# A three-layer interaction network in float32: the order of the first loads, and how the last eight samples are pooled

## The chip, the cores and the metric

The kernel runs on one core of one Trainium2 chip. The metric is the device time of one execution in microseconds (us); the time before is the median of three runs.

## The reference

The input `x` holds 1024 samples of 64 features by 16 embedding elements (`e`). Each of three layers multiplies every feature of `x` with every channel of the hidden state, element by element of `e`, and contracts all products with a weight matrix. Half of the outputs of layers 0 and 1 goes on as the hidden state, the other half to the end; there everything is added up over `e` and weighted with one vector into one number for each sample.

```python
x0 = h = x                                   # [1024, 64, 16]
for i in range(3):
    z = einsum('bfe,bge->bfge', x0, h).reshape(B, f0 * fh, 16)
    y = einsum('oc,bce->boe', W[i], z) + b[i][None, :, None]   # 128 outputs
    x_i, h = (y[:, :64], y[:, 64:]) if i < 2 else (y, y)
    xs.append(x_i)
pooled = sum(concatenate(xs, axis=1), axis=2)                  # [1024, 256]
return pooled @ fc_w.T + fc_b                                  # [1024, 1]
```

Since the end is linear, the kernel folds `fc_w` into the weights: `V2` (from `W2` and its part of `fc_w`), then `V1` and `V0`, and a constant. Each sample's result is a sum over 64 rows and 16 elements of products `uu`, plus the constant.

## The kernel before

**Tiling.** The samples are cut into 32 chunks of `CB = 32`; a chunk is `N = 512` columns, sample by sample with 16 elements each. Two chunks, an even and an odd one, share a pair `k`: the even one has rows 0 to 63, the odd one rows 64 to 127. For a chunk, `product` makes four tiles `z` (index `j`, [128, 4, 512]) by multiplying `xa` (x's rows, four shifts of them, 1 MB) with a column block of `x`, on VectorE (DVE), now and then on GpSimd (POOL). `contract` then runs 16 matmuls of [128 x 128] weights `w_all` with 512 columns into a PSUM accumulator, each of them two passes in float32. `factors` copies one half of the accumulator with ScalarE (ACT, L332) and multiplies it with the other half on DVE (L338) into `uu[:, 0]`; V0's part of the pair is `uu[:, 1]`, made earlier by `x_v0x`. `sums` (L347) adds `uu` over `e` into `acc` [128, 2, 16, 32], and `pool` adds `acc` over rows with a matmul whose stationary operand `ones` [128, 2] has one column for each half of the rows (L612).

**Order.** The order of each engine's instructions is the order of the program text; nothing is scheduled by a planner. Each engine works its list in that order, and so do the DMA queues of SP (SyncE) and ACT. Consecutive DMAs, of both queues, take eight completion semaphores in turn, so a DMA can only be issued when the one eight before it has landed.

**The head.** The weights of the third layer need layer 1's output of four chunks first (`HEAD = [2, 3, 0, 1]`, here `c0` to `c3`), and meanwhile the folded matrix is made from `W2` and `W1`. TensorE (PE) starts with matmuls on zeros (L106). All loads of the head are issued by SP: `xa` of c0 in a first quarter (two halves of 64 rows), a second quarter and the rest; `wh`, block 0 of W0 (`w0t[:, 0]`, 256 KB); the first quarter of c1; the other three blocks of W0 (`w0r`, L182, one block and then two); the vectors `vs` (L183, 100 KB); the rest of c1; then W2 in two halves of 1 MB (L188), W1 (L189) and c2.

- For c0 and c1 the second factor is not loaded but shifted out of `xa`'s first quarter by PE (`shift_pair`, L205). The pair (0, 1) reads the upper 64 rows for j = 0 and the lower 64 for j = 1.
- `h1_weights(j)` (L355) makes block j of `w_all` on DVE: it adds two halves of W0's block j, one of which ACT has copied to PSUM (L365 for block 0, L374 for block 1, L379 for blocks 2 and 3).
- c0's z of j = 1 is made by POOL in pieces, the others by DVE. DVE's order is: block 0 of the weights, z of j = 0 in pieces (i = 0, i = 1, i = 2 and 3), half of z of j = 2, block 1 of the weights, the rest of j = 2, blocks 2 and 3, z of j = 3.
- PE's order (`half_contract`, L298): tiles i = 0 and 1 of j = 0, c1's shifts (0, 3), tiles 2 and 3, j = 1, c1's shifts (1, 2), j = 2 and 3; then `pv` (L413), a product of W2 with `fv2` (32 copies of one column of `vs`, copied by ACT at L398), for each half of W2; then c1's contraction, of which the folded matrix `pm` (L437) is a neighbour.

**The tail.** The last chunk, 31, has its accumulator in two pieces: `CUT = 24` samples (384 columns) and 8 samples (128 columns). After the first piece its factors and sums run while PE contracts the second. After the second piece one chain of small steps follows: ACT's copy (L332), DVE's multiplication (L338), DVE's sum over e (L347), PE's pool (L612), DVE's addition of the constant `cst` (L623), and a DMA of the pair's 64 results by SP (L624).

Of the kernel before, what the change touches and what calls it, by code (L numbers as in the profile page):

```python
# [49 lines left out]
NCH = B // CB  # L50
NI = 4
NJ = 4
NT = NI * NJ
XR = 128 + NI
# [10 lines left out]
def cin_kernel(ctx, tc, xra, xrb, wh, w0r, w1h, w2t, wx1, wx0, vec, out):  # L65
    nc = tc.nc
# [22 lines left out]


    vs = const_tile("vs", [128, NV])
    fc2, bh1, bh2 = vs[:, 0:1], vs[:, 1:2], vs[0:64, 2:3]
    bcol, fcol, fcb = vs[:, 3:5], vs[:, 5:7], vs[:, 7:8]
    w0ds, fcr = vs[:, 8:72], vs[:, 72:200]

    fv2 = const_tile("fv2", [128, 32])

    v0w = const_tile("v0w", [128, 2, F])
    v1w = const_tile("v1w", [128, 2, F])
# [2 lines left out]


    zeros = nc.const_aps.tensor(0.0, [128, 128])
    for n in (128,) * 5 + (64,):
        nc.tensor.matmul(misc[:, 0:n], zeros, zeros[:, 0:n], start=True, stop=True)  # L106

    shift = const_tile("shift", [128, 96])
# [7 lines left out]
    ones = const_tile("ones", [128, 2])  # L116
# [9 lines left out]
    res = const_tile("res", [128, 128])  # L126


    xas, xbs, xxs, xrs, sqs = {}, {}, {}, {}, {}

    def load_xa(c, at=slice(0, NI), rows=slice(0, 128)):
        if at.start == rows.start == 0:
            xas[c] = xp.tile([128, NI, N], F32, tag="xa", name=f"xa_{c}")
        nc.sync.dma_start(  # L134
            out=xas[c][rows, at, :],
            in_=bass.AP(
                tensor=xra.tensor, offset=(c * XR + rows.start + at.start) * N,
                ap=[[N, rows.stop - rows.start], [1, (at.stop - at.start) * N]],
            ),
        )  # L140

# [29 lines left out]
    c0, c1, c2, c3 = HEAD  # L171
    w0t = z_tile("w0t")
    w2s = [flat_tile(f"w2_{k}") for k in range(2)]
    w1s = set_tile("w1s")
    for rows in halves:
        load_xa(c0, slice(0, 1), rows)
    nc.sync.dma_start(out=w0t[:, 0, :], in_=wh)  # L177
    load_xa(c0, slice(1, 2))
    load_xa(c0, slice(2, 4))
    load_xa(c1, slice(0, 1))  # L180
    for at in (slice(0, 1), slice(1, NJ - 1)):
        nc.sync.dma_start(out=w0t[:, at.start + 1 : at.stop + 1, :], in_=w0r[:, at])  # L182
    nc.sync.dma_start(out=vs, in_=vec)  # L183
    load_xa(c1, slice(1, 4))
    w0s = [w0t[:, j, :].rearrange("p (i v g) -> p i v g", v=2, g=F) for j in range(NJ)]
    xb_gps = xp.tile([128, NJ, N], F32, tag="xb", name="xb_gps")
# [20 lines left out]
                    xas[c][halves[r], 0, :], start=True, stop=True,  # L207
                )

    for j, tag in ((1, "y"), (0, "y"), (2, "set"), (3, "acc")):  # L210
        shifted(c0, j, tag)
    shift_pair(c0, (0, 1))
    shift_pair(c0, (2, 3))
# [31 lines left out]
    def tiles(j):  # L245

        return (1, 2, 3, 0) if j == NJ - 1 else range(NI)
# [42 lines left out]
                    )  # L290


    def half_contract(c, *js, last=None, at=None):
        for j in js:
            for i in at or tiles(j):
                t = j * NI + i
                for n in range(2):
                    nc.tensor.matmul(  # L298
                        accs[c][halves[n]], w_all[:, t, 0:64],
                        zs[c, j][:, i, n * H2 : (n + 1) * H2],  # L300
                        start=(t == 0), stop=(j == last and i == tiles(j)[-1]),
                    )
# [42 lines left out]
    def sums(k, rows=slice(0, 128), of=slice(0, 2), half=slice(0, CB)):  # L345

        nc.vector.tensor_reduce(  # L347
            acc[rows, of, k, half],
            uus[k][rows, of, E * half.start : E * half.stop].rearrange("p k (b e) -> p k b e", e=E),
            AX.X,  # L350
            ALU.add,
        )
# [27 lines left out]
    nc.vector.memset(w0o[3][SQ, 0, :], 0.0)  # L380
    for j in (2, 3):
        h1_weights(j, w0o[j])
    half_contract(c0, 0, at=(0, 1))


    for j, tag in ((0, "y"), (3, "acc"), (1, "y"), (2, "set")):
        shifted(c1, j, tag)
    shift_pair(c1, (0, 3))
    half_contract(c0, 0, at=(2, 3))
    half_contract(c0, 1)  # L390
    shift_pair(c1, (1, 2))
    new_acc(c1, H2)
# [2 lines left out]

    product(c0, 3)
    load_chunk(c3)
    nc.scalar.copy(fv2, fc2.to_broadcast([128, 32]))  # L398
    half_contract(c0, 2, 3, last=3)
    keep_h1(c0)  # L400

# [8 lines left out]
    for n in range(2):  # L410
        pv = ps.tile([128, 512], F32, tag=("set", "y")[n], name=f"pv2_{n}")
        for k in range(4):
            nc.tensor.matmul(  # L413
                pv[32 * k : 32 * k + 32], fv2, w2s[n][:, k * 512 : (k + 1) * 512],
                start=True, stop=True,
# [6 lines left out]
    for h in range(2):  # L422
        at = slice(32 * h, 32 * h + 32)
# [40 lines left out]
    for half, queue in enumerate((nc.sync, nc.scalar)):  # L464
        queue.dma_start(
            out=m_ap(0, 32 * half, [[row, F], [1, 32 * F]]), in_=m_rows[halves[half]]
# [5 lines left out]
        out=m_ap(64, 68, [[row, 4], [4 * F, 7], [1, 4 * F]]),  # L472
        in_=m_rows[0:4, 4 * F :].rearrange("p (k c) -> p k c", c=4 * F),
# [79 lines left out]
        head_q(0, j)  # L553

    cst = const_tile("cst", [128, 1])
    made = set()

    def load_products(c, other=None):
# [46 lines left out]
    NP = NCH // 2  # L605
    QP = NP // 4
# [7 lines left out]
            tile_position=(0, 32 * g), skip_group_check=True, **flags,  # L614
        )

    def finish(k0, k1, queue, engine=nc.scalar):
        g, at = k0 // QP, slice(k0 % QP, (k1 - 1) % QP + 1)
        rows = slice(32 * g, 32 * g + 2)
        if engine is nc.scalar:  # L620
            engine.activation(res[rows, at, :], po[rows, at, :], AF.Identity, bias=cst[rows])
        else:
            engine.tensor_scalar(res[rows, at, :], po[rows, at, :], cst[rows], None, ALU.add)  # L623
        queue.dma_start(out=outs[:, k0:k1, :], in_=res[rows, at, :])  # L624


# [1 line left out]
    for s, c in enumerate(order):  # L628
        k, head = c // 2, c in HEAD
        if order[s - 1] in HEAD and not head:  # L630
            for n in range(NF // 2):
                x_v0x(n)
            for n in HEAD:
                factors(n)
                if n % 2:
                    sums(n // 2)
        if 0 < s < len(order) - 2 and s not in (2, 3):
            load_products(*order[s + 2 : s + (4 if s == 6 else 3)])
        if s in (2, 3):

            if s == 2:
                for n in order[4:6]:
                    load_chunk(n)
                load_shared(0)
            for j in (0, 1) if s == 2 else (2, 3):
                for n in order[4:6]:
                    product(n, j)
        if s == len(HEAD) + 5:

            pc = ps.tile([128, 1], F32, tag="set", name="pc")  # L650
            for j in range(2):
                nc.tensor.matmul(
                    pc, fcol[:, j : j + 1].to_broadcast([128, 128]), bcol[:, j : j + 1],
                    start=(j == 0), stop=(j == 1),
                )
            nc.scalar.activation(cst, pc, AF.Identity, bias=fcb, scale=float(E))
        if not head:
            if c % 4 < 2:
                new_acc(c)
            if c == NCH - 1:  # L660
                factors(c - 1)
                sums(k, of=slice(1, 2))
                sums(k, slice(0, 64), slice(0, 1))
# [12 lines left out]
        elif c % 2:  # L676
            for n in (c - 1, c):
                new_acc(n)
            for j in range(NJ):
                head_q(k, j)  # L680
            contract_shared(0)
        if c % 4 == 1 and not head:
            for n in (1, 2):
                new_acc(c + n)
            contract_shared(c - 1)
        if s == 0:
            v0_weights()
            load_products(order[2], order[3])

        if c == HEAD[0] or c % 4 in (0, 3) and s and order[s - 1] not in HEAD and c < NCH - 1:  # L690
            factors(order[s - 1])
            if order[s - 1] % 2:
                sums(order[s - 1] // 2)
        elif c % 4 == 2 and not head:
            factors(c - 2)
            factors(c - 1)
            x_v0x(k - 1)
            x_v0x(k)
            sums(k - 1)


    first, last = slice(0, CUT), slice(CUT, CB)
    factors(NCH - 1)
    sums(NP - 1, slice(64, 128), slice(0, 1), first)
    for j in range(NJ):
        contract(NCH - 1, j, 1)
    factors(NCH - 1, slice(1, 2))
    sums(NP - 1, slice(64, 128), slice(0, 1), last)
    pool(NP - 1, NP, start=False, stop=True)
    finish(NP - 1, NP, nc.sync, nc.vector)  # L710


# [69 lines left out]
```

## Time and profile before

| what | value |
|---|---|
| time, median of 3 runs | 485.92 us (485.56 to 486.34) |
| time of the profiled execution | 485.56 us |
| span in its profile | 483.8 us |
| PE busy | 478.6 us, 99% of the span |
| DVE, ACT, POOL busy | 369.0, 67.0, 15.4 us |
| granted TensorE clock of the core, mean | 1.00 |
| data moved | 87.01 MB, 180 GB/s on average |

The profile shows one execution. Its span begins and ends with the program's instructions on the core; the rest of the execution's time, 485.56 - 483.8 = 1.8 us, lies around it. Times in the views count from the start of the span. A group "x8" of the timeline is eight instructions merged; "[0.60 <-DMA xa<-in_xra]" after one says that its engine was idle for 0.60 us before it and what ended that. A float32 matmul is recorded as two.

### The profile page before, as it was taken

The numbers are of one execution on the slowest core, as the hardware profiler recorded it, in microseconds if no ns is written. First come the engines' busy times: TensorE is split into PE (matmuls) and PEld (weight loads), VectorE is DVE, ScalarE is ACT, GpSimd is POOL, SyncE is SP. The second block draws the span as 40 slices with busy tenths as digits, with TensorE's granted clock in tenths as the row PEclk, the third lists the DMA queues.
The fourth block names the chain that finished last, engine by engine and source line by source line (L and its number), as shares of the span: only waits on it lengthen the run. The fifth ranks groups of instructions, "written<-read, shape, count | busy, mean of one in ns | idle before, by whom it ended". The sixth has DMA issues, their size and how long they took to land.

```text
span 483.8 us, 4411 instructions
## 1 busy us (share of the span) xinstructions
PE 478.6 (99%) x1800; PEld 215.4 (45%) x1800; DVE 369.0 (76%) x228; ACT 67.0 (14%) x141; POOL 15.4 (3%) x16
## 2 busy tenths in 40 slices
PE   8999999999999999999999999999999999999997
PEld 4465344443344444444444444444444444444555
DVE  4994799998899988898877686767878677771321
ACT  3242033111120111001000010001000010000001
POOL 5330000000000000000000000000000000000000
PEclk9999999999999999999999999999999999999999
DMA  7996996653951782587237344463346631000000
GB/s 279 415 310 196 389 384 261 229 205 120 354 234 75 239 293 108 198 268 280 110 128 215 159 173 173 152 211 110 136 173 208 225 127 49 0 1 0 0 1 1
DMA packets 19818, 87.01 MB, mean 180 GB/s; under 512 B 4850, under 2 KB 5522, under 8 KB 10902
## 3 DMA queue, kind: packets, MB, share of 16 engines
q1 hardware_dynamic: 18886, 85.81, 49.3%
q10 hardware_dynamic: 912, 0.92, 0.7%
q8 instruction: 14, 0.23, 0.2%
q14 instruction: 6, 0.05, 0.0%
HBM read 85.08 MB, written 1.64 MB: 179 GB/s over the span
## 4 chain that ended last, share of the span: by engine, by line
PE 95%; DMA 2%; SPq 1%; issue 0%; DVE 0%; ACT 0%
PE acc L257 80%; PE acc L316 6%; PE acc L298 4%; PE acc L273 3%; DMA w<-in_w2t 2%; PE acc L286 1%; SPq L134 1%; PE pm L437 0%; PE y L278 0%; PE pv L413 0%; SPq L182 0%; SPq L177 0%; PE po L612 0%; SPq L188 0%; SPq L183 0%
## 5 line engine op out<-in xcount | busy, mean ns | idle before, releaser
L257 PE MATMUL acc<-z,w_all 128*128 128x512 f32 (+2 forms) x928 | 387.6, 579 | 0.0
L235 DVE TENSOR_TENSOR z<-xa,xb 128x2048 f32<-128x2048 f32 x124 | 278.4, 2286 | 42.6 <-PE acc L257 36.3
L257 PEld LDWEIGHTS acc<-z,w_all 128*128 128x128 f32 x928 | 173.1, 190 | 213.0 <-issue 206.7
L240 ACT ACTIVATE z<-xa 32x512 f32<-32x512 f32 x34 | 21.3, 625 | 337.2 <-DVE z L235 335.2
L338 DVE SCALAR_TENSOR_TENSOR uu<-acc,vs,q 64x512 f32<-64x512 f32 (+2 forms) x29 | 21.2, 731 | 57.8 <-ACT q L332 57.6
L298 PE MATMUL acc<-z,w_all 128*64 128x256 f32 x256 | 28.8, 381 | 0.0
L316 PE MATMUL acc<-z,w_all 128*64 128x512 f32 x128 | 27.9, 593 | 0.0
L332 ACT COPY q<-acc 64x512 f32<-64x512 f32 (+2 forms) x33 | 18.7, 566 | 35.9 <-PE acc L257 19.8
L298 PEld LDWEIGHTS acc<-z,w_all 128*64 128x64 f32 x256 | 18.0, 137 | 11.8 <-issue 1.6
L235 DVE TENSOR_TENSOR z<-xa,xp 128x2048 f32<-128x2048 f32 (+2 forms) x12 | 20.4, 1749 | 0.6 <-DMA xa<-in_xra 0.6
L347 DVE TENSOR_REDUCE acc<-uu 128x64 f32<-128x1024 f32 (+4 forms) x19 | 20.3, 1073 | 0.3
L316 PEld LDWEIGHTS acc<-z,w_all 128*64 128x64 f32 x128 | 9.1, 137 | 18.0 <-issue 17.9
L278 PE MATMUL y<-xr,v0w 32*64 32x512 f32 x128 | 15.9, 600 | 0.0
L273 PE MATMUL acc<-xr,v1w 32*64 32x512 f32 (+2 forms) x132 | 15.7, 587 | 0.0
L343 DVE SCALAR_TENSOR_TENSOR uu<-y,cx,xx 128x512 f32<-128x512 f32 x16 | 11.3, 747 | 0.2
L235 POOL TENSOR_TENSOR z<-xa,xb_gps 128x512 f32<-128x512 f32 (+2 forms) x4 | 9.4, 2379 | 5.8 <-ACT xb_gps L367 4.9
L273 PEld LDWEIGHTS acc<-xr,v1w 32*64 32x64 f32 x132 | 5.1, 131 | 10.0 <-issue 9.8
L286 PE MATMUL acc<-sq,w_sq 32*64 32x512 f32 (+2 forms) x132 | 8.7, 574 | 0.0
L205 PE MATMUL xp<-xa,shift 64*64 64x512 f32 x32 | 5.8, 762 | 0.7 <-DMA xa<-in_xra 0.6
L165 ACT ACTIVATE sq<-xr 128x512 f32<-128x512 f32 x8 | 5.0, 630 | 3.0 <-DMA xr<-in_xra 2.8
L286 PEld LDWEIGHTS acc<-sq,w_sq 32*64 32x64 f32 x132 | 3.7, 132 | 3.7 <-issue 3.5
L355 DVE TENSOR_TENSOR w_all<-w0t,w0p 128x256 f32<-128x256 f32 x2 | 0.8, 419 | 5.8 <-ACT w0p L365 5.8
(57 smaller groups left out, 67.9 us busy)
## 6 DMA issues: line engine op xcount, KB each, us to landing
xa<-in_xra SPq DMA_DIRECT2D x32, 1024.0 KB, 5.0
xb<-in_xrb SPq DMA_DIRECT2D x31, 1024.0 KB, 7.3
xr<-in_xra SPq DMA_DIRECT2D x32, 128.0 KB, 7.7
xx<-in_xra SPq DMA_DIRECT2D x32, 128.0 KB, 7.7
w<-in_w2t SPq DMA_DIRECT2D x2, 1024.0 KB, 10.5
w1s<-in_w1h SPq DMA_DIRECT2D x1, 1024.0 KB
w1x<-in_wx SPq DMA_DIRECT2D x1, 1024.0 KB
w0x<-in_wx SPq DMA_DIRECT2D x1, 1024.0 KB, 5.5
```

The lines of the kernel that those rows point to most:

```text
L235: engine.tensor_tensor(zs[c, j][:, at, :], xas[c][:, at, :], xbs[c][j].unsqueeze(1).to_broadcast([128, last - first, N]), ALU.mult,)
L240: nc.scalar.activation(zs[c, j][SQ, 0, :], xas[c][SQ, 0, :], AF.Square)
L257: nc.tensor.matmul(acc_c, w_all[:, t, w_cols(c)], zs[c, j][:, i, cols], start=(t == 0 and c % 4 < 2), stop=(t == NT - NI and c % 4 >= 2),)
L273: nc.tensor.matmul(acc_c[halves[1 - n]], v1w[at, m], xr[:, cols], start=(m == 0 and c not in ends), stop=False, tile_position=(at.start, 6 ...
L278: nc.tensor.matmul(ys[c // 2][halves[n]], v0w[at, m], xr, start=(m == 0), stop=(m == 1), tile_position=(at.start, 64 * n),)
L286: nc.tensor.matmul(acc_c[halves[n]], w_sq[at, w_cols(c)][:, 64 * n : 64 * n + 64], sqs[first][at, cols], start=h and (first == 0 or c not ...
L298: nc.tensor.matmul(accs[c][halves[n]], w_all[:, t, 0:64], zs[c, j][:, i, n * H2 : (n + 1) * H2], start=(t == 0), stop=(j == last and i == ...
L316: nc.tensor.matmul(accs[c][halves[1 - c % 2]], w_all[:, t, 64:128], zs[c, j][:, i, :], start=(t == 0), stop=False,)
L332: nc.scalar.copy(q[h, cols], acc_c[64 - h.start : 128 - h.start])
L338: nc.vector.scalar_tensor_tensor(uu[:, cols], acc_c[h], bh1[h], q[h, cols], ALU.add, ALU.mult)
L343: nc.vector.scalar_tensor_tensor(uu_tile(k)[:, 1, :], ys[k], cx, xxs[k], ALU.add, ALU.mult)
L347: nc.vector.tensor_reduce(acc[rows, of, k, half], uus[k][rows, of, E * half.start : E * half.stop].rearrange("p k (b e) -> p k b e", e=E), ...
```

## The change

In the head:

- the vectors are loaded by ACT's DMA queue as the program's first DMA, and ACT's copy of `fv2`, which waits for them, becomes ACT's first copy (before: vectors on SP's queue behind W0, the copy behind c0's z);
- x's first quarter is loaded by one DMA in place of two, and W0's blocks 1 to 3 by one in place of two;
- one more matmul on zeros of 128 columns;
- PE contracts all four tiles of c0's j = 0 ahead of c1's shifts (0, 3), in place of two before them and two behind.

In the tail:

- rows 64 to 127 of `acc` for the last 8 samples are set to zero by POOL, so that the last `pool` holds only 24 samples of chunk 31. It no longer waits for the second piece. ACT adds the constant, and the pair's results go out in two DMAs: the even chunk's 32, and the odd chunk's first 24;
- the last 8 samples go another way: three matmuls with one stationary column add `uu[:, 1]` (V0's part), the constant (`csl`, the constant divided by 128 * 16, made once by ACT) and last `uu[:, 0]` over the rows, for 128 columns, into a [1, 128] accumulator `pl`; DVE then adds `pl` over e into 8 results, and a third DMA writes them.

```diff
     vs = const_tile("vs", [128, NV])
+    nc.scalar.dma_start(out=vs, in_=vec)
...
     fv2 = const_tile("fv2", [128, 32])
+    nc.scalar.copy(fv2, fc2.to_broadcast([128, 32]))
...
-    for n in (128,) * 5 + (64,):
+    for n in (128,) * 6 + (64,):
         nc.tensor.matmul(misc[:, 0:n], zeros, zeros[:, 0:n], start=True, stop=True)
...
-    for rows in halves:
-        load_xa(c0, slice(0, 1), rows)
+    load_xa(c0, slice(0, 1))
     nc.sync.dma_start(out=w0t[:, 0, :], in_=wh)
     load_xa(c0, slice(1, 2))
     load_xa(c0, slice(2, 4))
     load_xa(c1, slice(0, 1))
-    for at in (slice(0, 1), slice(1, NJ - 1)):
-        nc.sync.dma_start(out=w0t[:, at.start + 1 : at.stop + 1, :], in_=w0r[:, at])
-    nc.sync.dma_start(out=vs, in_=vec)
+    nc.sync.dma_start(out=w0t[:, 1:NJ, :], in_=w0r)
     load_xa(c1, slice(1, 4))
...
-    half_contract(c0, 0, at=(0, 1))
+    half_contract(c0, 0)
...
     shift_pair(c1, (0, 3))
-    half_contract(c0, 0, at=(2, 3))
     half_contract(c0, 1)
     shift_pair(c1, (1, 2))
...
     load_chunk(c3)
-    nc.scalar.copy(fv2, fc2.to_broadcast([128, 32]))
...
+    csl = const_tile("csl", [128, 1])
+    nc.gpsimd.memset(acc[64:128, 0, NCH // 2 - 1, CUT:], 0.0)
...
             nc.scalar.activation(cst, pc, AF.Identity, bias=fcb, scale=float(E))
+            nc.scalar.activation(csl, cst, AF.Identity, scale=1.0 / (128 * E))
...
-    first, last = slice(0, CUT), slice(CUT, CB)
+    first, last = slice(0, CUT), slice(E * CUT, N)
     factors(NCH - 1)
     sums(NP - 1, slice(64, 128), slice(0, 1), first)
     for j in range(NJ):
         contract(NCH - 1, j, 1)
     factors(NCH - 1, slice(1, 2))
-    sums(NP - 1, slice(64, 128), slice(0, 1), last)
     pool(NP - 1, NP, start=False, stop=True)
-    finish(NP - 1, NP, nc.sync, nc.vector)
+    pl = ps.tile([1, N - E * CUT], F32, tag="acc", name="pl", bufs=4)
+    uu = uus[NP - 1]
+    nc.tensor.matmul(pl, ones[:, 1:2], uu[:, 1, last], start=True, stop=False)
+    nc.tensor.matmul(
+        pl, csl, nc.const_aps.tensor(1.0, [128, N - E * CUT]), start=False, stop=False
+    )
+    nc.tensor.matmul(pl, ones[:, 1:2], uu[:, 0, last], start=False, stop=True)
+    rows, (even, odd) = slice(96, 98), (outs[0:1, NP - 1], outs[1:2, NP - 1])
+    nc.scalar.activation(
+        res[rows, QP - 1], po[rows, QP - 1], AF.Identity, bias=cst[rows]
+    )
+    nc.sync.dma_start(out=even, in_=res[96:97, QP - 1])
+    nc.sync.dma_start(out=odd[:, first], in_=res[97:98, QP - 1, first])
+    rl = hb[0:1, 0, 0 : CB - CUT]
+    nc.vector.tensor_reduce(rl, pl.rearrange("p (b e) -> p b e", e=E), AX.X, ALU.add)
+    nc.sync.dma_start(out=odd[:, CUT:], in_=rl)
```

More of the change, by code (lines that the diff above doesn't have):

```diff
@@ L129, in cin_kernel, with load_xa @@
     xas, xbs, xxs, xrs, sqs = {}, {}, {}, {}, {}
-    def load_xa(c, at=slice(0, NI), rows=slice(0, 128)):
-        if at.start == rows.start == 0:
+    def load_xa(c, at=slice(0, NI)):
+        if c not in xas or at.start == 0:
             xas[c] = xp.tile([128, NI, N], F32, tag="xa", name=f"xa_{c}")
         nc.sync.dma_start(
-            out=xas[c][rows, at, :],
+            out=xas[c][:, at, :],
             in_=bass.AP(
-                tensor=xra.tensor, offset=(c * XR + rows.start + at.start) * N,
-                ap=[[N, rows.stop - rows.start], [1, (at.stop - at.start) * N]],
+                tensor=xra.tensor, offset=c * XR * N + at.start * N,
+                ap=[[N, 128], [1, (at.stop - at.start) * N]],
             ),
@@ L208, in shift_pair @@
                 )
-    for j, tag in ((1, "y"), (0, "y"), (2, "set"), (3, "acc")):
+    for j, tag in enumerate(("y", "y", "set", "acc")):
         shifted(c0, j, tag)
@@ L290, in contract_shared, with half_contract @@
                     )
-    def half_contract(c, *js, last=None, at=None):
+    def half_contract(c, *js, last=None):
         for j in js:
-            for i in at or tiles(j):
+            for i in tiles(j):
                 t = j * NI + i
@@ L615, in pool, with finish @@
         )
-    def finish(k0, k1, queue, engine=nc.scalar):
+    def finish(k0, k1, queue):
         g, at = k0 // QP, slice(k0 % QP, (k1 - 1) % QP + 1)
         rows = slice(32 * g, 32 * g + 2)
[L620 to L623, printed above, removed]
+        nc.scalar.activation(
+            res[rows, at, :], po[rows, at, :], AF.Identity, bias=cst[rows]
+        )
         queue.dma_start(out=outs[:, k0:k1, :], in_=res[rows, at, :])
@@ L707, in cin_kernel @@
     factors(NCH - 1, slice(1, 2))
-    sums(NP - 1, slice(64, 128), slice(0, 1), last)
     pool(NP - 1, NP, start=False, stop=True)
-    finish(NP - 1, NP, nc.sync, nc.vector)
+    pl = ps.tile([1, N - E * CUT], F32, tag="acc", name="pl", bufs=4)
[6 more added lines that the diff above has]
+    rows, (even, odd) = slice(96, 98), (outs[0:1, NP - 1], outs[1:2, NP - 1])
+    nc.scalar.activation(
+        res[rows, QP - 1], po[rows, QP - 1], AF.Identity, bias=cst[rows]
+    )
+    nc.sync.dma_start(out=even, in_=res[96:97, QP - 1])
[3 more added lines that the diff above has]
+    nc.sync.dma_start(out=odd[:, CUT:], in_=rl)
 def kernel(r_x, L0_rec_W0, L0_rec_b0, L0_rec_W1, L0_rec_b1, L0_rec_W2, L0_rec_b2, L0_rec_fc_w, L0_rec_fc_b):
```

## The prediction

> **What bounds the kernel.** The page says at once what counts: PE is busy all through.
>
> ```profile
> PE 478.6 (99%) x1800; PEld 215.4 (45%) x1800; DVE 369.0 (76%) x228; ACT 67.0 (14%) x141; POOL 15.4 (3%) x16
> ```
>
> So I asked where PE still waits. The list of PE's waits between 19.5 and 480 us is empty, and the starts of its matmuls show no hole there. A gain or loss of the change must therefore lie before 19.7 us or after 480.1 us, and whatever PE gains by 19.7 us comes through whole. In the timeline of PE I read the head:
>
> ```profile
> 7.21 1.08 PE L298 MATMUL acc<-z,w_all 128*64 128x256 f32 x8
> 8.90 1.09 PE L205 MATMUL xp<-xa,shift 64*64 64x512 f32 x8 [0.60 <-DMA xa<-in_xra]
> 9.91 2.88 PE L298 MATMUL acc<-z,w_all 128*64 128x256 f32 x24
> 12.73 1.09 PE L205 MATMUL xp<-xa,shift 64*64 64x512 f32 x8
> ...
> 17.35 1.07 PE L413 MATMUL pv<-w,fv 128*32 128x512 f32 x8
> 18.72 1.07 PE L413 MATMUL pv<-w,fv 128*32 128x512 f32 x8 [0.30 <-DMA w<-in_w2t]
> ```
>
> PE has little to do until 9.9 us and is full from there, but for W2's second half, which lands at 18.6. A half of `pv` takes 0.91 us (its eight passes begin every 0.43 to 0.45 us in fours), so PE would have been ready at 17.35 + 0.91 = 18.26 and lost 18.72 - 18.26 = 0.46 us. Behind 9.91 the eight instructions of tiles 2 and 3 end at 10.6; j = 1 begins at 10.85, when block 1 of the weights is there. Its chain is in ACT's and DVE's timelines:
>
> ```profile
> 9.49 0.38 ACT L374 COPY w0p<-w0t 128x256 f32<-128x256 f32 x1 [2.48 <-DMA w0t<-in_w0r]
> 10.72 0.79 ACT L379 COPY misc<-w0t 128x256 f32<-128x256 f32 x2 [0.85 <-DMA w0t<-in_w0r]
> ```
> ```profile
> 10.29 0.42 DVE L355 TENSOR_TENSOR w_all<-w0t,w0p 128x256 f32<-128x256 f32 x1
> ```
>
> Block 1 lands at 9.43, blocks 2 and 3 at 10.71. What the DMAs do meanwhile is in the DMA view of the first 40 us (1 us a column):
>
> ```profile
> DMA  0057999999999999999999999999987979974037
> GB/s 0 0 154 217 377 342 350 229 401 419 415 444 408 459 418 418 426 434 410 426 418 383 338 438 426 438 434 410 442 246 164 246 238 279 205 229 162 14 64 179
> ```
>
> From 4 us to 28 us they are full: landings go by bytes, not by issue times. Between 2.2 us (first packet) and 4.5 us they are not: by half microseconds the packets fill 0.14 of 0.28, then 0.37, 0.35, 0.38 and 0.44 of 0.50 us, so 0.6 us of transfer time is unused, because SP issues one DMA per 0.62 us there. Last, the tail, in the chain of waits:
>
> ```profile
> 480.42 0.37 DVE uu L338
> 480.79 0.02 issue
> 480.81 0.29 DVE acc L347
> 481.11 0.14 issue
> 481.24 0.23 PE po L612 x2
> 481.47 0.03 issue
> 481.50 0.26 DVE res L623
> ```
>
> **Head: loads.** SP's issues in front of W0's rest fall from six to five, and x's quarter and `wh` reach the DMAs one issue (0.62 us) earlier; the vectors come in parallel from ACT. So the unused 0.6 us can be filled; between none and all, I take all, as 356 KB (x's quarter and the vectors) wait at the first packet in place of 128. The vectors' 128 packets of 800 bytes took 38 ns each, on 16 engines 8 x 0.038 = 0.30 us. They lie now ahead of W0's rest. So W0's rest comes 0.6 - 0.3 = 0.3 us earlier (bounds: 0.6, if the vectors fit where nothing else was ready, and -0.3, if nothing is filled), everything behind the vectors' old place, W2 included, 0.6 us earlier (bounds 0 and 0.6). The merged SP issues cost nothing more than that: SP's later issues wait for landings anyway.
>
> [...]
>
> **Head: block 1 as the gate.** With one DMA, block 1 can be used only when all three have landed: 10.71 - 0.3 = 10.41 in place of 9.43. Then ACT's copy (0.02 + 0.38) and DVE's addition (0.03 + 0.42) and 0.04 to PE: j = 1 begins at 10.41 + 0.89 = 11.30, 0.45 later than now. DVE stands in order: behind block 1 wait the rest of z of j = 2, blocks 2 and 3, z of j = 3 and c1's. All slip by some 0.5 us; z of j = 3 would end at 15.4 and PE wants it at 15.6, and `pv`'s copies end at 23.7 where PE wants them at 25.0: covered. Now j = 1 takes 12.73 - 10.85 = 1.88 us, with short waits for POOL's pieces; sixteen pairs at 0.108 us are 1.73 us, and POOL, which starts at 6.7 in place of 7.15 (both j are shifted at once), is no longer late. So c1's second shifts begin at 13.03, 0.30 later, and the rest of PE's work up to `pv` follows without a hole, 0.30 later. PE is ready for W2's second half at 18.56; that lands at 18.0. c1's contraction starts 18.72 - 18.56 = 0.16 us earlier: **-0.16**. The ends: W0's rest 0.6 early gives -0.46; 0.3 late gives 11.9, ready at 19.16, and +0.44.
>
> Before the gate: c1's shifts move behind tiles 2 and 3, whose z waits for x's second half (landing at 8.01, now some 7.7) and ends at 8.95; tiles and shifts (0.75 + 0.95) end at 10.7, before 11.30. If the gate opened earlier, this would be the next bound.
>
> **Head: small things at nothing.** One more zero matmul is two passes of 0.2135 us: PE is free at 4.0 in place of 3.58. Now the second half of x's quarter lands at 4.39. The whole quarter, begun at 2.2 with 16 packets an engine (8 x 84 + 8 x 38 ns = 1 us, slow packets 0.3, 0.4 until the waiter sees it), lands at 3.7 to 4.0. `fv2` at ACT's head waits for the vectors, some 4.0, behind it the copy of block 0, which needs `wh` at 4.5 to 5; if the vectors came at 5.5, block 0 would be 0.5 late, while tile 2 still waits for x until 8.9. Without both covers it would cost its 0.22 us and the wait.
>
> **Tail.** Removed behind L338: DVE's sum and DVE's addition of the constant. From the end of L338 to the DMA issue it is 0.03 + 0.28 + 0.15 + 0.22 + 0.04 + 0.26 + 0.03 = 1.01 us. New: 0.15 to PE, one matmul of 128 columns, 0.04, DVE's sum over 128 of PSUM, 0.03. The matmul: a pass of 128 columns takes 0.245 to 0.27 and the second begins 0.08 to 0.11 after it, so 0.35 against 0.22 for 32 columns. The sum: from SBUF 128 elements took 0.282 us; with PSUM and a scalar operand (L338) 0.356; a product with one PSUM source (128x512, L235) took 0.682, about 0.533 + 0.15, as one without; I take 0.30, near the reduction, and keep both ends. Sum: 0.15 + 0.35 + 0.04 + 0.30 + 0.03 = 0.87, so **-0.13** (-0.21 with 0.10 to PE and 0.282; 0.00 with 0.36 and 0.43 for the matmul, its passes one fully behind the other).
>
> [...]
>
> The other two matmuls into `pl` (four passes of 0.107) and the pool run while ACT and DVE make L332 and L338 (480.13 to 480.78): hidden, and without cover 0.45 us. ACT's addition for the pair takes at most 0.33:
>
> ```profile
> L621 ACT ACTIVATE res<-po,cst 2x96 f32<-2x96 f32 x1 | 0.3, 333 | 0.0
> ```
>
> It starts at 480.42 behind L332; SP's two issues (0.25 and 0.05 between) end at 481.4, the last DMA is wanted at 481.66. The landing of the last DMA and the end behind it (481.79 to 483.78) stay. `csl` costs ACT 0.26 us once at 191 us and POOL's zeros some 0.1 us, on engines 14% and 3% busy: nothing.
>
> **Sum.** -0.16 - 0.13 = -0.29 us: the profiled execution, 485.56, would be 485.27. It is the fastest of three, 0.36 under their median; on the median, 485.92 - 0.29 = **485.63 us**.
>
> **Rivals.**
> 1. *The gate closes later (slower).* Mechanism: W0's merged DMA holds block 1, DVE's queue and PE's j = 1. Break-even is at a landing of 10.57 (11.46 for j = 1, 18.72 for `pv`); from there every microsecond is lost whole. With the vectors ahead and nothing filled (11.01) the head is +0.44: 485.92 + 0.44 - 0.13 = 486.23. Over 0.97 us it needs 11.7. For it: packets up to 1.08 us long at 5 and 7 us in this trace. Against: the idle DMAs before 4 us.
> 2. *The DMAs gain fully (faster).* W0 0.6 early, j = 1 at 11.0, head -0.46, tail -0.21: 485.25. More than that PE's own work (10.7) and W2 at 18.0 forbid.
> 3. *The tail does not do what it says.* If ACT's addition came so late that the two DMAs end after 481.7, SP becomes the bound: 0.3 us for each issue, tail +0.2, head -0.16: 485.96. Against it: ACT has nothing else there.
>
> **How the numbers follow.** What a measurement of this kernel can tell from no change is about 0.2%, 0.97 us; the three runs themselves spread over 0.78. Forecast 50%, rival 1 24% (a third of it beyond 0.97), rival 2 16%, rival 3 10%. Beyond 0.97 faster nothing here reaches; I leave 6% for it, and 9% for slower. So faster 0.06, same 0.85, slower 0.09. Range: both ends of head and tail together (-0.67 and +0.44), and 0.3 for the scatter of a median, less than half of the runs' spread: 484.95 to 486.7.
>
> **What would show it.** ACT's L374 near 10.4 with no wait between it and L379; j = 1 of c0 at 11.3; no hole in front of the second `pv`; c1's contraction at 19.55; first shift at 4.0; 0.87 us between L338 and the last issue. Wrong if L374 is behind 10.6, if the vectors' landing delays L365, or if PE shows a new wait behind 20 us.

## The result, and the profile after

The changed kernel took 484.70 us (median of six executions, 484.61 to 485.05), the kernel before 486.34 us beside it: ratio 0.9970, interval 0.9957 to 0.9983, so 1.64 us faster, clear of noise. The forecast was 485.63 us with a range from 484.95; the time lies outside it, by 0.25 us. The profiled execution took 484.75 us with a span of 483.0 us.

The two profiles differ by 0.81 us. The rest of the 1.64 lies in the medians: before's profiled execution (485.56) is 0.78 us under its own median (486.34), and after's (484.75) is 0.05 above its own. These 0.83 us turned out to be the larger part of the story.

PE's timeline of the head after. Line numbers are a little lower than before's: L204 are the shifts, L297 is `half_contract`, L410 is `pv`.

```profile
7.23 1.08 PE L297 MATMUL acc<-z,w_all 128*64 128x256 f32 x8
8.76 1.08 PE L297 MATMUL acc<-z,w_all 128*64 128x256 f32 x8 [0.44 <-DVE z L234]
9.77 1.09 PE L204 MATMUL xp<-xa,shift 64*64 64x512 f32 x8
10.79 1.95 PE L297 MATMUL acc<-z,w_all 128*64 128x256 f32 x16
...
17.29 1.92 PE L410 MATMUL pv<-w,fv 128*32 128x512 f32 x16
19.15 1.73 PE L297 MATMUL acc<-z,w_all 128*64 128x256 f32 x13
```

The hole in front of the second half of `pv` is gone, and c1's contraction starts at 19.15 in place of 19.72: -0.57 us. j = 1 of c0 begins at 10.79, directly behind c1's shifts; W0's rest was no gate here. ACT's timeline shows why (L373 copies block 1, L378 blocks 2 and 3):

```profile
9.70 0.38 ACT L373 COPY w0p<-w0t 128x256 f32<-128x256 f32 x1 [2.77 <-DMA w0t<-in_w0r]
10.01 0.78 ACT L378 COPY misc<-w0t 128x256 f32<-128x256 f32 x2
```

All three blocks were there at 9.64, not at the forecast 10.41. x's second half came earlier too: in before DVE waits for it until 8.02 us, in after DVE goes through z of j = 0 without waiting for it. And in the DMA view, one column for each microsecond, the loads run at 394 to 442 GB/s from 3 to 20 us, without the dip to 229 GB/s that before has in its eighth column:

```profile
DMA  0159999999999999999999999999199899850058
GB/s 0 16 178 394 416 397 414 414 424 418 424 442 410 434 418 401 442 401 410 418 344 416 438 444 422 418 401 393 66 262 188 238 287 197 229 223 18 5 156 195
```

The tail, in the chain of waits (L337 multiplies, L715 is the last matmul into `pl`, L723 the sum over e):

```profile
479.85 0.37 DVE uu L337
480.22 0.04 issue
480.26 0.39 PE pl L715 x2
480.65 0.02 issue
480.68 0.28 DVE hb L723
```

From the end of the multiplication to the issue of the last DMA it is 0.78 us (480.21 to 480.98) in place of 1.01.

### The profile page after: what moved, and what is told of

The parts are those of the page before. It is cut to its first block, busy times and chain, and to the rows that moved or that the text cites. A ratio compares the mean times of both kernels' runs of the same rounds, so it can differ in the third digit from the quotient of the medians.

```text
span 483.0 us, 4429 instructions
## 1 busy us (share of the span) xinstructions
PE 478.9 (99%) x1808; PEld 215.6 (45%) x1808; DVE 368.6 (76%) x227; ACT 67.5 (14%) x143; POOL 15.4 (3%) x17
## 3 DMA queue, kind: packets, MB, share of 16 engines
HBM read 85.08 MB, written 1.64 MB: 180 GB/s over the span
## 4 chain that ended last, share of the span: by engine, by line
PE 98%; DMA 1%; DVE 1%; issue 0%; ACT 0%
PE acc L256 80%; PE acc L315 6%; PE acc L297 6%; PE acc L272 3%; PE acc L285 1%; PE xp L204 1%; DMA xa<-in_xra 1%; DVE z L234 1%; PE pm L434 0%; PE pv L410 0%; PE y L277 0%; PE pl L715 0%; DVE uu L337 0%; PE pc L651 0%; PE po L612 0%
## 5 line engine op out<-in xcount | busy, mean ns | idle before, releaser
L337 DVE SCALAR_TENSOR_TENSOR uu<-acc,vs,q 64x512 f32<-64x512 f32 (+2 forms) x29 | 21.2, 731 | 58.0 <-ACT q L331 57.8
L297 PE MATMUL acc<-z,w_all 128*64 128x256 f32 x256 | 28.9, 381 | 0.4 <-DVE z L234 0.4
L297 PEld LDWEIGHTS acc<-z,w_all 128*64 128x64 f32 x256 | 17.8, 137 | 12.7 <-DVE z L234 2.0
L346 DVE TENSOR_REDUCE acc<-uu 128x64 f32<-128x1024 f32 (+3 forms) x18 | 20.0, 1117 | 0.3
L533 DVE TENSOR_TENSOR w_all<-ms 128x256 f32<-128x256 f32 x4 | 1.5, 424 | 5.4 <-DMA ms<-md 5.4
L204 PE MATMUL xp<-xa,shift 64*64 64x512 f32 x32 | 5.2, 754 | 0.3 <-DMA xa<-in_xra 0.3
```

What stands on the lines that cost most here:

```text
L297: nc.tensor.matmul(accs[c][halves[n]], w_all[:, t, 0:64], zs[c, j][:, i, n * H2 : (n + 1) * H2], start=(t == 0), stop=(j == last and i == ...
L337: nc.vector.scalar_tensor_tensor(uu[:, cols], acc_c[h], bh1[h], q[h, cols], ALU.add, ALU.mult)
L346: nc.vector.tensor_reduce(acc[rows, of, k, half], uus[k][rows, of, E * half.start : E * half.stop].rearrange("p k (b e) -> p k b e", e=E), ...
```

## The experiments

Medians in us, with the kernel before run beside each group. Each group ran on one chip: the first (to head_vs_behind) on chip 7, the second (to order_only) on chip 3, the last three on chip 2, so that from the third repeat of the changed kernel on the place was the same. The chip of the result's comparison is not on record. "c1" is the start of c1's contraction in the run's profile, "profiled" the time of that one execution. "Two" is W0's rest in two DMAs.

| run | median | before beside it | ratio, 95% interval | c1 | profiled |
|---|---|---|---|---|---|
| before_again | 486.21 | 486.41 | 0.9998 (0.9986 to 1.001) | 20.30 | 486.19 |
| head_only | 485.66 | 486.41 | 0.9985 (0.9976 to 0.9994) | 19.90 | 485.72 |
| tail_only | 486.25 | 486.41 | 0.9999 (0.9989 to 1.0009) | 20.54 | 486.26 |
| head_vs_behind | 485.82 | 486.41 | 0.9987 (0.9978 to 0.9996) | 19.19 | 485.01 |
| after_again | 485.94 | 486.14 | 0.9995 (0.9985 to 1.0006) | 21.45 | 487.08 |
| vs_only | 486.29 | 486.14 | 1.0004 (0.9993 to 1.0016) | 19.39 | 485.25 |
| w0r_only | 486.60 | 486.14 | 1.0009 (0.9999 to 1.0019) | 20.42 | 486.20 |
| order_only | 487.10 | 486.14 | 1.0012 (0.9998 to 1.0025) | 21.84 | 487.72 |
| after_third | 485.90 | 486.13 | 0.9999 (0.9987 to 1.0011) | 19.90 | 485.61 |
| after_order | 485.76 | 486.13 | 0.9990 (0.9981 to 1.0000) | 19.96 | 485.72 |
| after_w0r2 (two) | 485.34 | 486.13 | 0.9982 (0.9974 to 0.9990) | 19.76 | 485.43 |
| after_both (two) | 485.49 | 486.13 | 0.9984 (0.9976 to 0.9993) | 20.05 | 485.90 |
| after_fourth | 485.69 | 485.93 | 0.9990 (0.9981 to 1.0000) | 20.47 | 486.08 |
| after_hold | 485.86 | 485.93 | 0.9997 (0.9984 to 1.0009) | 20.36 | 485.95 |
| w0r2_hold (two) | 485.88 | 485.93 | 0.9996 (0.9984 to 1.0008) | 20.36 | 486.03 |
| w0r2_again (two) | 485.67 | 485.93 | 0.9988 (0.9976 to 1.0001) | 20.14 | 485.82 |
| after_fifth | 485.70 | 486.08 | 0.9992 (0.9982 to 1.0001) | 19.75 | 485.49 |
| after_quarters | 484.89 | 486.08 | 0.9975 (0.9965 to 0.9985) | 19.16 | 484.89 |

One reading goes through the whole table: profiled time minus c1's start is 465.78 to 465.89 us in every kernel with before's tail and 465.59 to 465.85 in every one with the new tail. Whatever differs between these profiled executions happens before c1's contraction, but for the tail, which is 0.15 us on average (465.84 against 465.69).

**The parts.** before_again is the kernel before, unchanged.

> The kernel before, unchanged, for a second profile. The forecast had the change at -0.29 us, by its profile against the first profile of before it is -0.81, by the medians -1.64. Theory A (before's start is unsteady: its DMAs are disturbed by a different amount in each execution, and the profiled one of before was a lucky one): times from 485.5 to 486.7 us, and a profile in which W0's second block or W2's second half lands at another time than 9.43 and 18.60 us, with c1's contraction at 19.7 to 20.6 us in step with the time. Theory B (the 0.8 us lie outside the span): c1's contraction again at 19.7 us and a span of 483.8 us whatever the time.

Same time as before (486.21 against 486.41), and a profile that looks otherwise:

```profile
19.31 1.06 PE L413 MATMUL pv<-w,fv 128*32 128x512 f32 x8 [0.34 <-DMA w<-in_w2t]
20.30 0.44 PE L298 MATMUL acc<-z,w_all 128*64 128x256 f32 x2
```

c1's contraction starts at 20.30, and the time is 0.63 us above that of the first profile. Theory A holds: the head is unsteady, and the first profile was a lucky one.

head_only has all edits of the head, tail_only all edits of the tail.

> The head of the change alone: vectors on ACT's queue and their copy first, x's quarter and W0's rest in one DMA each, one more zero matmul, all four tiles of j = 0 ahead of c1's shifts; the tail of before. Theory A: -0.57 us against the profile of before, c1's contraction at 19.15 us, and -1.2 to -1.4 us by the medians, with times that scatter by less than 0.5 us. Rival (the tail brings more than the 0.24 us that its steps show): no more than -0.6 us by the medians.

> The tail of the change alone, the head of before. Theory A: -0.24 us in the steps behind the last multiplication (0.78 us from its end to the last DMA's issue in place of 1.01), so -0.2 to -0.3 us by the medians, hidden in the scatter of the head of before. Rival (the tail brings more): -0.8 us or more. The forecast for these steps was 0.87 us.

The head alone brings -0.75 us by the medians, short of A's -1.2 and beyond the rival; W0's rest landed at 10.5 us, not at 9.64. The tail brings -0.16 by the medians, which its interval does not tell from nothing; in the steps it is 0.78 against 1.01 us, as read. Together they fall short of -1.64.

head_vs_behind is head_only with the vectors back on SP and their copy back in its old place:

```diff
-    nc.scalar.dma_start(out=vs, in_=vec)
     nc.sync.dma_start(out=w0t[:, 1:NJ, :], in_=w0r)
+    nc.sync.dma_start(out=vs, in_=vec)
...
```

> The head of the change, but with the vectors on SP's queue behind W0's rest and their copy where before has it; the tail of before. It tells the vectors from the merged loads. Theory A1 (the DMAs are filled early because x's quarter and W0's rest need fewer issues): c1's contraction at 19.1 to 19.3 us and -1.1 us or more by the medians, as with the whole head. Theory A2 (the vectors on ACT's queue fill the idle DMAs): c1's contraction within 0.2 us of before's, and -0.3 us at most.

-0.59 us, within the intervals the same as the head with the vectors on ACT. So the gain does not need the vectors' move (A1, though smaller than it said). Which of the other edits carries it stays open: of those, W0's rest in one DMA and PE's order each lose when they stand alone (w0r_only and order_only below), and no run has x's first quarter in one DMA, or the zeros, alone.

**Single edits, and the changed kernel again.**

> The changed kernel, unchanged, for a second profile beside the parts. Head alone gave -0.75 us by the medians (485.66 against 486.41) and tail alone -0.16. Theory S (the parts add up, and the first comparison of the whole, -1.64, was helped by a head that ran undisturbed each time): about -0.9 to -1.0 us, 485.4, with c1's contraction between 19.1 and 19.9 us. Theory I (head and tail gain from each other): again -1.6 us, 484.8. Theory P (whether the DMAs run at full rate from 2.5 us on differs by the place, not by the kernel): the head's landings as in head_only (W0's rest at 10.5 us), in place of 9.64.

-0.20 us in place of -1.64: theory P, or worse. The profiled execution was one of two in twelve at 487.1, and it shows a second loss that nothing in the forecast had. The table by stages of after_again's profile: the window, its length, busy us (and instructions) of PE, PEld, DVE, ACT and POOL, the granted clock, the share of the DMAs, and GB/s:

```profile
8.00:9.00 1.00, 0.00 (x0) 0.00 (x0) 0.83 (x1) 0.00 (x0) 1.00 (x2) 1.00 1.06 438
9.00:10.00 1.00, 0.56 (x6) 0.41 (x8) 1.00 (x2) 0.00 (x0) 1.00 (x2) 1.00 1.01 418
10.00:11.00 1.00, 1.00 (x10) 0.38 (x10) 0.52 (x1) 0.22 (x1) 0.98 (x1) 0.73 1.04 436
11.00:12.00 1.00, 1.00 (x8) 0.00 (x0) 0.81 (x2) 0.83 (x3) 0.00 (x0) 0.50 1.03 434
12.00:13.00 1.00, 1.00 (x8) 0.44 (x6) 0.95 (x3) 0.46 (x1) 0.00 (x0) 0.50 0.97 410
13.00:14.00 1.00, 1.00 (x8) 0.56 (x6) 1.00 (x3) 0.12 (x1) 0.80 (x1) 0.56 1.02 426
```

PE stood idle while z of tiles 2 and 3 was late, and the clock went to a half for 3.4 us, in which c1's shifts and j = 1 ran.

vs_only has only the vectors' move, w0r_only only W0's rest in one DMA, order_only only the order of PE's work. order_only's edit:

```diff
-    half_contract(c0, 0, at=(0, 1))
+    half_contract(c0, 0)
 ...
     shift_pair(c1, (0, 3))
-    half_contract(c0, 0, at=(2, 3))
     half_contract(c0, 1)
```

> Before, with the vectors on ACT's queue first and their copy as ACT's first; nothing else. The forecast's terms: 0.30 us of the vectors' packets leave the place ahead of c1's rest and W2, so W2's second half lands 0.3 us or more earlier, which takes up to 0.46 us of the wait in front of the second half of pv: -0.2 to -0.4 us. Rival (the head copy waits and delays ACT, or x's quarter is late because the vectors' packets lie between): c1's contraction as before or later, 0 to +0.3 us.

+0.15 us, which the interval does not tell from nothing: the rival by the median. In its profile, its fastest execution, the wait in front of the second half of `pv` is gone and c1 starts at 19.39, as the forecast's terms have it; the twelve executions (485.25 to 487.75) scatter too much to show such a gain.

> Before, with W0's blocks 1 to 3 in one DMA; nothing else. The forecast's gate: block 1 is used when all three have landed, 1.28 us after it now does, so j = 1 of c0 begins 0.7 to 0.8 us later (11.6 in place of 10.85 us in the profile), and of this 0.46 us are taken by the wait in front of the second half of pv: +0.1 to +0.3 us. Rival (one issue fewer makes everything behind it earlier): -0.2 us or less.

+0.46 us by the medians (the interval touches 1): the gate's side, dearer than its expectation. Its profile does not show the gate alone: the full clock came at 9.57 us there, in before's at 6.35, and PE's first tiles began at 8.44 in place of 7.21.

> Before, with all four tiles of c0's j = 0 ahead of c1's shifts; nothing else. PE would wait for z of tiles 2 and 3 (9.24 us in the profile) and put c1's shifts (0.95 us) behind: j = 1 begins at 9.28 + 0.75 + 0.95 = 11.0 in place of 10.85, all of it inside the 0.46 us in front of pv: 0 to +0.1 us. Rival (c1's shifts waited for a landing that comes later than that z): -0.1 us or less.

+0.96 us by the medians, against an expected 0 to +0.1. Four of its twelve executions had a mean granted clock of 0.995 or 0.996, its profiled one among them, with the same half clock from 11 to 14.5 us. The clock is one part of the price of the order: the other eight, at full clock, still have a median of 486.64, 0.50 above before's, and no profile shows where they lose that.

**Undoing gate and order in the changed kernel.** after_order restores before's order, after_w0r2 W0's rest in two DMAs, after_both does both.

> The changed kernel, unchanged, a third time, beside its variants. So far -1.64 us in the first comparison and -0.2 in the second, where two of twelve executions had a granted clock of 0.996 and took 1.2 us more. Theory P (what the head gains depends on how undisturbed the DMAs run between 4 and 8 us in that place): between -0.2 and -1.6 us, and in the profile W0's rest lands at 9.6 us with -1.6, at 10.5 or later with -0.2 to -0.7. Rival (one number holds everywhere and the comparisons scatter): about -0.8 us with landings as in the first profile of after.

> The changed kernel with before's order of PE's work: tiles 0 and 1 of c0's j = 0, c1's shifts (0, 3), tiles 2 and 3. Theory C (all four tiles first leave PE idle from 7 to 9.4 us, and where a window of 3.4 us holds too little work the clock falls to a half for 3.4 us): no execution with a granted clock under 0.998, c1's shifts at 8.2 to 9 us at full clock, and the median 0.1 to 0.4 us under the changed kernel's, its slowest execution 1 us under the changed kernel's slowest. Rival (the order costs nothing in most executions, as W0's rest is the gate behind it): median within 0.1 us of the changed kernel's.

> The changed kernel with W0's rest in two DMAs again, block 1 and then blocks 2 and 3. The forecast's gate: block 1 lands 1.2 us earlier, so j = 1 of c0 begins behind c1's shifts at once (0.4 to 0.7 us earlier than with one DMA where W0's rest lands at 10.5 us, nothing where it lands at 9.7). Median 0.1 to 0.5 us under the changed kernel's by the gate; the rival (c1's shifts, behind tiles 2 and 3, are the bound, and the gate is not): within 0.1 us.

> The changed kernel with both: before's order of PE's work, and W0's rest in two DMAs. If gate and order are the two losses inside the change, this is the fastest: 0.4 to 0.8 us under the changed kernel's median, j = 1 of c0 at 10.3 to 10.8 us, and the second half of pv waits for W2 again. If the landing of W2 is the next bound, it is no better than the better one of the two by more than 0.1 us.

after_third: -0.23 us, W0's rest at 10.5 us; four of twelve executions at a mean clock of 0.996 took 487.2 to 487.5 us, all others at most 486.2. after_order: none of twelve under 0.998, its slowest 486.87; 0.14 us under after_third by the medians; theory C has that and the clock, but its slowest is 0.6 us under after_third's slowest, not 1. With before's order PE has nothing else in front of j = 1, and waits for block 1, which ACT copies at 10.63:

```profile
11.61 1.95 PE L297 MATMUL acc<-z,w_all 128*64 128x256 f32 x16 [0.72 <-DVE w_all L354]
```

That is the gate. In the changed kernel's own order it is smaller, as two pairs of timelines show; by the medians after_w0r2 is 0.56 us under after_third. First ACT's of after_third, one DMA:

```profile
10.57 0.38 ACT L373 COPY w0p<-w0t 128x256 f32<-128x256 f32 x1 [4.03 <-DMA w0t<-in_w0r]
10.88 0.78 ACT L378 COPY misc<-w0t 128x256 f32<-128x256 f32 x2
```

and PE's of the same kernel:

```profile
10.28 1.09 PE L204 MATMUL xp<-xa,shift 64*64 64x512 f32 x8
11.54 1.95 PE L297 MATMUL acc<-z,w_all 128*64 128x256 f32 x16 [0.18 <-POOL z L234]
```

Then ACT's of after_w0r2, two DMAs:

```profile
9.06 0.38 ACT L374 COPY w0p<-w0t 128x256 f32<-128x256 f32 x1 [3.33 <-DMA w0t<-in_w0r]
10.28 0.78 ACT L379 COPY misc<-w0t 128x256 f32<-128x256 f32 x2 [0.84 <-DMA w0t<-in_w0r]
```

and PE's of that one:

```profile
9.95 1.09 PE L205 MATMUL xp<-xa,shift 64*64 64x512 f32 x8
10.97 1.95 PE L298 MATMUL acc<-z,w_all 128*64 128x256 f32 x16
```

With one DMA, block 1 comes 1.5 us later, and PE stands some 0.24 us between shifts and j = 1; with two, j = 1 follows at once. The gate is not all of these 0.24: the view puts the end of the wait down to POOL's z, and DVE had block 1 ready at 11.40, 0.14 us before j = 1 began. The rest of the 0.57 us by which j = 1 starts earlier with two DMAs is x's second half: tiles 2 and 3 begin at 8.94 there, at 9.26 with one. after_both is no better than after_w0r2 (485.49 and 485.34): W2's second half is the bound again (`pv` waits until 19.05 us in its profile), the last clause of its expectation.

**Where the dip comes from.** In every later profile slow packets stand among x's and W0's loads, in after_third nine of 4096 bytes with 0.93 to 1.15 us each at 4.8 to 5.2 us (0.16 us is the usual time of one), and the DMA view shows the hole, 209 GB/s in the sixth column:

```profile
GB/s 0 29 213 389 346 209 389 342 422 418 428 424 442 410 434 410 442 401 418 410 389 410 432 403 446 410 434 410 246 41 156 262 131 336 221 172 325 56 0 77
```

after_hold and w0r2_hold keep W2, W1 and c2 from being issued until ACT has copied c0's shifted tile:

```diff
     xbs[c0][1] = xb_gps[:, 0, :]
+    nc.scalar.copy(w2s[0][0:1, 0:1], xb_gps[0:1, 0, 0:1])
+    for k in range(2):
+        nc.sync.dma_start(out=w2s[k], in_=w2t[k])
...
```

> The changed kernel, but W2, W1 and c2 are not issued before ACT has copied c0's shifted tile (about 6 to 7 us in place of 4.1 us); ACT writes one element of W2's tile for that, nothing is left out. Theory D1 (the slow packets between 4 and 7.5 us come from issuing W2's DMAs while eight others are under way): no packet over 0.4 us among x's and W0's, W0's rest lands at 9.7 us in place of 10.5, and 0.5 to 0.8 us under the changed kernel's median, scatter as in the first place. Theory D2 (the disturbance comes from outside the kernel's issues): slow packets as before, W0's rest at 10.5 us, and the median within 0.2 us of the changed kernel's.

> The same hold, with W0's rest in two DMAs. By D1: 0.3 to 0.6 us under the version with two DMAs and no hold. By D2: the same as that version, 0.4 to 0.6 us under the changed kernel.

W2 is issued at 6.9 us in both, and the slow packets stand at 4.5 to 5.4 us all the same, the longest 1.74 us. D1 has fallen. Each is 0.2 us slower than its partner below, which its interval does not tell from nothing.

> The changed kernel, unchanged, in a fourth place. It gave -1.64, -0.20 and -0.23 us by the medians. Theory P (the first place ran its loads undisturbed, the others do not): around -0.2 to -0.3 us with packets of 0.5 us or more among x's and W0's loads between 4 and 7.5 us; or around -1.6 us and no such packets. Rival (the difference lies elsewhere than in the loads): -1.6 us with such packets, or -0.2 us without.

> The changed kernel with W0's rest in two DMAs, again, in another place. It gave 485.34 us against 485.90 of the changed kernel and 486.13 of before. If the gate is the loss inside the change: 0.4 to 0.7 us under the changed kernel where W0's rest lands at 10.5 us, and within 0.2 us of it where it lands at 9.7. No execution with a granted clock under 0.998.

after_fourth: -0.24 us, with slow packets and W0's rest copied at 11.13: theory P's first branch. w0r2_again: 485.67, the same as after_fourth, not 0.4 to 0.7 under it, and one execution at a clock of 0.996. The pair with the hold gives nothing either (485.88 with two DMAs, 485.86 with one): two DMAs are worth 0.0 to 0.6 us, not a fixed sum. In w0r2_again's profile W2's second half is the bound (19.14 us), 0.4 later than in after_w0r2.

after_quarters loads the second half of c0's x, in which the slow packets stand, in two:

```diff
-    load_xa(c0, slice(2, 4))
+    load_xa(c0, slice(2, 3))
+    load_xa(c0, slice(3, 4))
```

> The changed kernel, unchanged, a fifth time. By now -1.64, -0.20, -0.23 and -0.24 us. Theory P: -0.2 to -0.3 us where the profile has slow packets (0.5 us and more) among x's and W0's loads between 4 and 7.5 us, -1.6 us where it has none. Rival: a time that does not go with the packets.

> The changed kernel with the second half of c0's x (the packets of 4096 bytes, among which the slow ones stand in every later profile) loaded in two DMAs of 2048-byte packets; nothing is left out. Holding W2's issue back did not remove the slow packets, so theory D1 has fallen. Theory E (the shape of this transfer makes them): no packet over 0.4 us between 4 and 7.5 us, W0's rest at 9.7 us, 0.4 to 0.7 us under the changed kernel. Theory D2 (they come from outside): the slow packets stand at the same time, now among those of 2048 bytes, and the median is within 0.2 us of the changed kernel's.

after_fifth: -0.38 us. after_quarters: -1.19 us, 0.81 under the changed kernel beside it, and its executions lie between 484.67 and 485.42 where after_fifth's lie between 484.70 and 487.24. This is one comparison, and the two intervals still meet (0.9982 to 0.9985). The time goes as theory E says, the packets do not: between 4.8 and 6.3 us seven packets of 2048 bytes take over 0.4 us, 0.57 at most. The hole in its DMA view is nearly closed:

```profile
GB/s 0 50 216 369 379 340 377 412 424 406 412 463 426 410 418 459 401 393 418 434 383 422 416 426 410 442 418 377 98 147 246 139 328 213 197 255 134 0 112 173
```

W0's rest is copied at 9.83 us, c1's contraction starts at 19.16 as in the first profile of after, and none of nine executions had a lowered clock. It is the fastest version of the experiments, 0.9975 of before.

Slow packets are not the whole hole. From 4 to 6 us, in order: the first profile of after, after_third and after_fifth (columns as in the table by stages above; the last two are the DMAs' share and GB/s):

```profile
4.00:6.00 2.00, 1.72 (x9) 0.61 (x12) 0.42 (x1) 0.58 (x2) 0.00 (x0) 1.00 1.03 407
4.00:6.00 2.00, 1.94 (x13) 0.77 (x16) 0.52 (x2) 0.64 (x3) 0.00 (x0) 1.00 1.00 278
4.00:6.00 2.00, 1.76 (x16) 0.60 (x16) 0.71 (x2) 1.18 (x3) 0.00 (x0) 1.00 0.79 268
```

In after_third the DMAs are full and slow; in after_fifth they stand idle for a fifth of the time (share 0.79) though the loads have been issued, and only three of x's packets there take over 0.4 us. What makes either, and why the first comparison's executions of the changed kernel ran undisturbed without the edit of after_quarters (484.61 to 485.05), is not settled; after_fifth's fastest two, at 484.70 and 484.83, show that it can happen. Whether it was the chip can't be told.

## Why the prediction was wrong

**Right.** No gain or loss arises between 19.7 and 480 us, and PE's position at c1's contraction is the head's whole account. The merged DMA of W0's rest is a gate for block 1 (after_order, where PE waits 0.72 us for it). W0's rest was expected at 10.41, and the later profiles of the changed kernel have 10.4 to 11.1; the sum of -0.29 us fits its four later comparisons: -0.20, -0.23, -0.24 and -0.38. No run tells the cost of the vectors' move from nothing; the addition on ACT was done at 480.12 us, and the last DMA was not held up on SP's queue. The zeros were hidden in the result's profile, where the first shift waits for x (0.28 us); in after_quarters the chain that ends last runs through them, so they are not free in every execution.

**The step that failed: the landing of W0's rest and x, taken as one number.** The result lies 1.35 us beyond the forecast's -0.29: 0.41 of it in the head between the two profiles, 0.11 in the tail between them, and 0.83 in the base, the step from the profiled execution to the median. The head and the base fail for the same reason. I put W0's rest 0.3 us earlier, 0.6 at best. In the execution behind the result it came 1.07 us earlier (10.71 to 9.64); of x's and W0's packets there only one took over 0.4 us (0.53), of the vectors' four (0.59 to 0.79, begun at 1.8 to 2.1 us). So j = 1 began at 10.79 where the sum has 11.30, PE came to `pv` 0.06 us earlier than before where the sum has 0.30 later, and the wait in front of its second half went whole. I had seen before's packets of up to 1.08 us and used them only against the rival of a late gate; that they could be absent after, and were part of before's 10.71, was not in the sum. The limit that rival 2 names (j = 1 behind PE's own tiles, at 10.7) is what the profile shows, at 10.79, with -0.57 in place of -0.46.

**The base.** I carried the difference of a sum made on before's profiled execution over to the median. That execution had a short head: c1 at 19.72 us, where before_again's is at 20.30. Adding the sum to the median assumes that the changed kernel's executions would lie as far above the best head as before's do; the six of the result did not. The run-to-run scatter, which I took for 0.3 us of measurement, is a property of the head. It is not smaller in the changed kernel: those six lie within 484.61 to 485.05, but all 54 of its executions within 484.61 to 487.48, as before's within 485.17 to 488.36. So the 1.64 us are 0.57 head and 0.24 tail between the profiles, 0.78 by which before's median lies above its profile, and 0.05 by which after's lies under its own. That the first comparison met such a head six times in six is not explained by the change: in the four later comparisons the same kernel gained 0.20 to 0.38. What made it stays open.

**Missing: the clock.** The forecast put tiles 2 and 3 ahead of c1's shifts at nothing as long as the gate came later. order_only shows what that overlooks: the shifts were the only work in a hole of some 2 us (PE waits 2.02 us for z there in its profile), and without them a lowered clock came more often: with before's order of PE's work 6 of 232 executions of the experiments had a mean clock under 0.998, with the new order 17 of 140.

**Mis-sized: the tail.** -0.13 forecast, -0.23 in the steps, just beyond my end of -0.21; over all profiles 0.15 us of it reach the time. The wait to PE is 0.05 us in place of 0.15 (in before, a separate wait and a load of weights of 0.03 stand there), and DVE's sum of 128 elements from PSUM takes 0.278 us, no more than the 0.282 from SBUF.

## What to carry to other kernels

Before a change is priced at tenths of a microsecond, look at what the scatter of the executions is made of: here it lay in the first 20 us, in when the loads land and in the clock, and one lucky profile hid it. Repeat the comparison before a gain of 0.3% is believed: -1.64 us came once, -0.20 to -0.38 four times. A merged load saves an issue but can be a gate for its first user; here that cost 0.0 to 0.6 us. Small work that fills a hole in PE's start can be worth more than its own time: with c1's shifts in the hole 6 of 232 executions had a mean clock under 0.998, with the new order 17 of 140.

## What was not expected of the hardware

- In the profiles of after_again and order_only the clock was at a half for 3.41 us each, from 10.5 and 11.1 us on; in the 3.41 us before that PE was busy for 0.42 and 0.41 of the time. The length of PE's hole alone does not decide it: PE waited for z for 1.99 and 2.02 us there, and for 2.19 us in head_only, whose clock stayed at 1.00. The first full clock came at 6.35 us in before's profile, at 6.50 in after's and at 9.57 in w0r_only's.
- Of 54 executions of the changed kernel eight had a mean clock of 0.996, and each of those took 486.78 us or more.
- Single DMA packets of the first loads can take many times their usual time: up to 1.74 us with 4096 bytes (usual 0.16, after_hold), 1.04 with 2048 (usual 0.08, before_again), 1.00 with 6144 (usual 0.23, w0r_only). So they do not belong to one size. x's second half has rows of 4096 bytes that begin 2048 bytes apart in the source; loaded as two DMAs of 2048-byte rows it had 0.57 at most and the time was 0.81 us shorter, in one comparison. Whether the shape does it, and what makes a packet slow, stays open.
